# A selective scan's last states: B, C and the scan's outputs placed in the room of K and V

## The chip, the cores and the metric

The kernel runs on one core of one Trainium2 chip, as one launch. The metric is the device time of that core in microseconds (us); where several runs were made, the median is given. The profile is of one separate execution, with its own time.

## What is computed

Two layers run one after the other on x of shape (4, 128, 64, 64), 4 images of 128 channels and 4096 pixels. The first is an attention of 4 heads over the 4096 pixels of an image, with a residual and a layer norm. The second adds three things: a 3 x 3 convolution, a product in the Fourier domain, and a Mamba block, which is where the change lies. Cut to what matters here:

```
y = layernorm(x + softmax(Q K^T / sqrt(32)) V Wo + bo)      # per image, 4 heads of 32
xs = silu(conv1d(in_proj(y)));  dt, B, C = split(x_proj(xs)); dt = softplus(dt_proj(dt))
h0 = 0                                                       # per image, 256 channels x 16 states
h  = exp(dt * A) * h + dt * B * xs                           # pixel after pixel, 4096 of them
y' = sum over the 16 states of (h * C) + xs * D
out = conv3x3(y) + fourier(y) + out_proj(y' * silu(z))
```

## The kernel before

**Tiles and stages.** An image's 4096 pixels are cut into 8 chunks of 512 (`NCH`, `L`), so there are 32 chunks (`CHUNKS`). The attention works on halves: one chunk of queries with one pair of heads, 64 of them (`HALVES`), each against 32 tiles of 128 keys (`NT`). The outer loop at L985 counts steps t; half H takes steps 32 H to 32 H + 31, so the attention ends at t = 2048. In each step it issues the matmuls of one key tile: `scores_for_exp` (L478, reads K), `scores_for_max` for the next half (L434, reads K), `times_values` (L498, reads V).

**The order of the work.** All else is fitted in between by hand. Short jobs (generators) are due at given steps, and a `Plan` (L100) lets so many of them advance in each step; after the attention it lets up to four of each kind. The order of instructions on each engine is therefore fixed when the kernel is built; each engine takes its own in order and waits by semaphores for the others. DMAs of the attention and the scan are issued by SP, also in order.

**K and V.** `KK` (L311) holds 2 x 8 tiles of 128 x 512, one per pair of heads and chunk, and `VA` (L314) 8 tiles of 128 x 528. They are reloaded for each image, and after step 2048 nothing uses them.

**The scan.** It runs `LAG` = 144 steps behind: chunk c starts at t = 144 + 64 c. A chunk has 32 states v: n = v // 2 is the state's number in the reference (0 to 15), hf = v % 2 the half of the 256 channels. Each takes two steps:
- `scan_load` (L769) brings rows n of B and of C, broadcast over the 128 partitions, from the DRAM tile `bcd` that `scan_bc` (L694) wrote: one DMA of 512 KB into `bc`, of which there are three buffers. It is issued three n ahead (L1012).
- `scan_decay` (L774), ACT: dA = exp(dt * A), into PSUM. In the tail two PSUM buffers take turns.
- `scan_input_term` (L782): db = u * B, on POOL (GpSimd) during the attention, on DVE (VectorE) after it. It stands two states ahead of its scan.
- `scan_state` (L787): the scan itself on DVE (L793), from `state` into one of two `hs` buffers; a copy of its last column to `state` on POOL (L796); the product with C on POOL (L797), in place; then the sum over n. For most chunks POOL adds into `acc` (L812). For the last two chunks (30 and 31), which lie after the attention, PE adds with an identity matmul into PSUM (L806).

`mamba_input` (L619) begins a chunk; at an image's first chunk it sets `state` and the convolution's `carry` to zero on POOL. In the instruction order that memset stands among the states of the chunk before it. `scan_output` (L890) gates the sums, multiplies by the output weights (L914), adds (L920) and, for the second half of an image, adds the flipped Fourier part that `load_flipped` brought (`wr`; additions L887, L888 on POOL). `flips` (L932) does this addition later for the first half of an image, with loads of `ob` and `wr` and a store; for the last image these four (chunks 27 to 24) fall into the tail.

**The tail.** After step 2048 there remain the last states of chunk 29, all of chunks 30 and 31 (t = 2064 to 2191), chunk 31's whole input side (`mamba_input`, `scan_dt`), two gates, a convolution (L857), three `scan_output` and the four flips.

Of the kernel before, what the change touches and what calls it, by code (L numbers as in the profile page):

```python
# [9 lines left out]
F32 = mybir.dt.float32  # L10
F32R = mybir.dt.float32r
AF = mybir.ActivationFunctionType
ALU = mybir.AluOpType
# [4 lines left out]
P = 128  # L18
# [5 lines left out]
L = 512  # L24
# [3 lines left out]
NH = DI // P  # L28
NS = 16
# [126 lines left out]
def attention_then_conv_mamba(  # L156
# [17 lines left out]
    nc = tc.nc  # L174
    ctx.enter_context(tc.manual_schedule())
    B, C, N = x.shape
    NCH = N // L
    NT = N // P
    CHUNKS = B * NCH
    HALVES = CHUNKS * PAIRS  # L180
    SCALE = float(HD) ** -0.5

    const = ctx.enter_context(tc.tile_pool(name="const", bufs=1))
    att = ctx.enter_context(tc.tile_pool(name="att", bufs=2))
    loc = ctx.enter_context(tc.tile_pool(name="loc", bufs=2))
# [9 lines left out]
    for h in range(HEADS):  # L195
        k, j = divmod(h, 2)
# [3 lines left out]
    for h in range(HEADS):  # L200
        k, j = divmod(h, 2)
        c = COL["bk"] + k
# [9 lines left out]
    for h in range(HEADS):  # L212
        k, j = divmod(h, 2)
        c = COL["bq"] + h
# [16 lines left out]
    for h in range(HEADS):  # L231
        row = h % 2 * HS
        hs = slice(h * HD, (h + 1) * HD)
# [19 lines left out]
    def col(name, k=0):  # L253
        return vec[:, COL[name] + k : COL[name] + k + 1]
# [5 lines left out]
    sel = const.tile([P, P], F32R, name="sel")  # L260
    ones = const.tile([P, 1], F32, name="ones")
    nc.vector.memset(ones, 1.0)
    minus_one = const.tile([P, 1], F32, name="minus_one")
    nc.vector.memset(minus_one, -1.0)
    g = const.tile([P, 3, P], F32, name="g")
# [10 lines left out]
    def constants_of_the_rest():  # L276
# [34 lines left out]
    KK = [  # L311
        [const.tile([P, L], F32R, name=f"K_{k}_{i}") for i in range(NCH)] for k in range(PAIRS)
    ]
    VA = [const.tile([P, TPC, HEADS, HD + 1], F32, name=f"V_{i}") for i in range(NCH)]  # L314
# [4 lines left out]
    state = const.tile([P, NH * NS], F32, name="state")  # L319
# [5 lines left out]
    plan = Plan(2, {"x": 2, "f": 1})  # L325

    def bank_tile(bank, shape, name):
        return psum.tile(shape, F32, tag=f"m{bank}", name=name)
# [285 lines left out]
    xps, xss, dts, us, accs, gates, xds, bcds = ({} for _ in range(8))  # L614

    def inner(c):
        return xps[c][:, 1 : RPC + 1, 1 : W + 1]

    def mamba_input(c):  # L619

        i = c % NCH
        while c not in XH:
            yield ""
        yield ""
        xp = loc.tile([P, RPC + 2, W + 2], F32, tag="xp", name=f"xp_{c}", bufs=2)
        xps[c] = xp
        nc.gpsimd.memset(xp[:, :, 0 : W + 2 : W + 1], 0.0)
        if i == 0:
            nc.gpsimd.memset(xp[:, 0, 1 : W + 1], 0.0)
            nc.gpsimd.memset(state, 0.0)  # L630
            nc.gpsimd.memset(carry, 0.0)
        if i == NCH - 1:
            nc.gpsimd.memset(xp[:, RPC + 1, 1 : W + 1], 0.0)
        bank = yield "PB"
        pt = bank_tile(bank, [P, TPC, P], f"pt_{c}")
        for t in range(TPC):
            nc.tensor.transpose(pt[:, t, :], XH[c][:, t, :], ident)
        yield "A"
        plan.release(bank)
        nc.scalar.activation(  # L640
            inner(c),
            pt.rearrange("p t (r w) -> p (t r) w", w=W),
            AF.Identity,
            scale=col("gamma"),
            bias=col("beta"),
        )
        if i:
            nc.scalar.activation(xp[:, 0, 1 : W + 1], xps[c - 1][:, RPC, 1 : W + 1], AF.Copy)
            nc.scalar.activation(xps[c - 1][:, RPC + 1, 1 : W + 1], xp[:, 1, 1 : W + 1], AF.Copy)
            edges.add(c - 1)  # L650
        if i == NCH - 1:
            edges.add(c)

        xss[c], dts[c], us[c] = {}, {}, {}
        for hf in range(NH):
            plan.now(1, scan_input(c, hf))
        plan.now(2, spectral(c))
# [108 lines left out]

    dA, db, bcs, scaled = {}, {}, {}, set()

    def scan_load(c, n):  # L769
        bc = loc.tile([P, 2, L], F32, tag="bc", name=f"bc_{c}_{n}", bufs=3)  # L770
        nc.sync.dma_start(bc, bcds[c][n::NS, :].partition_broadcast(P))
        bcs[c, n] = bc

    def scan_decay(c, v):  # L774
        n, hf = divmod(v, NH)
# [6 lines left out]
    def scan_input_term(c, v, engine):  # L782
        n, hf = divmod(v, NH)
        db[c, v] = loc.tile([P, L], F32, tag="db", name=f"db_{c}_{hf * NS + n}")
        engine.tensor_tensor(db[c, v], us[c][hf], bcs[c, n][:, 0, :], ALU.mult)  # L785

    def scan_state(c, v):  # L787

        n, hf = divmod(v, NH)
        k = hf * NS + n  # L790
        assert (c, hf) in scaled
        hs = loc.tile([P, L], F32, tag="hs", name=f"hs_{c}_{k}")
        nc.vector.tensor_tensor_scan(  # L793
            hs, dA.pop((c, v)), db.pop((c, v)), state[:, k : k + 1], ALU.mult, ALU.add
        )
        nc.gpsimd.tensor_copy(state[:, k : k + 1], hs[:, L - 1 :])  # L796
        nc.gpsimd.tensor_tensor(hs, hs, bcs[c, n][:, 1, :], ALU.mult)  # L797
        if c >= CHUNKS - 2:

            if v == 0:  # L800
                late = psum.tile([P, NH, L], F32, tag=f"s{CHUNKS - c}", name=f"acc_{c}")
                for h in range(NH):
                    accs[c, h] = late[:, h, :]
            if n == 0:
                nc.tensor.matmul(accs[c, hf], ident, xss[c][hf], start=True, stop=False)
            nc.tensor.matmul(accs[c, hf], ident, hs, start=False, stop=n == NS - 1)  # L806
        elif n == 0:
            acc = loc.tile([P, L], F32, tag=f"acc{hf}", name=f"acc_{c}_{hf}")
            accs[c, hf] = acc
            nc.gpsimd.tensor_tensor(acc, xss[c][hf], hs, ALU.add)  # L810
        else:
            nc.gpsimd.tensor_tensor(accs[c, hf], accs[c, hf], hs, ALU.add)  # L812
# [3 lines left out]
    def spectral(c):  # L816

        b, i = divmod(c, NCH)
        bank = yield "PB"
        p1 = bank_tile(bank, [P, TPC, P], f"p1_{c}")  # L820
        for t in range(TPC):
            nc.tensor.matmul(p1[:, t, :], XH[c][:, t, :], hilbert, start=True, stop=True)
        yield "A"
        plan.release(bank)
        hx = loc.tile([P, L], F32, tag="hx", name=f"hx_{c}", bufs=2)
        hxs[c] = hx
        nc.scalar.activation(
            hx, p1.rearrange("p t c -> p (t c)"), AF.Copy, scale=col("gamma")
        )
        bank = yield "PB"  # L830
        pw = bank_tile(bank, [P, RPC, W], f"pw_{c}")
        nc.tensor.matmul(pw, g_flip, inner(c), start=True, stop=False)
        yield "P"
        nc.tensor.matmul(
            pw.rearrange("p r w -> p (r w)"), g_fliphil, hx, start=False, stop=True
        )
        yield "A"
        plan.release(bank)
        w = loc.tile([P, L], F32, tag="w", name=f"w_{c}", bufs=1)
        nc.scalar.activation(w, pw.rearrange("p r w -> p (r w)"), AF.Copy)  # L840
        yield ""
        if i == 0:
            wd[b] = dram.tile([P, N], F32, tag="wd", name=f"wd_{b}")
        nc.sync.dma_start(wd[b][:, i * L : (i + 1) * L], w)
# [136 lines left out]
            plan.at((b + 1) * NCH * SLOT + 44 + 10 * i, 4, flips(b * NCH + NCH // 2 - 1 - i))  # L981

    t = 6 - SLOT
    end = (CHUNKS + 3) * SLOT
    while t < end or not plan.idle():  # L985
        H, m = divmod(t, NT)
        if 0 <= H < HALVES:
            scores_for_exp(H, m)
        h1, s1 = divmod(t + LEAD, NT)
        if 0 <= h1 + 1 < HALVES:  # L990
            scores_for_max(h1 + 1, s1)
        H, m = divmod(t - 1, NT)
        last = m == NT - 1
        if last and 0 <= H < HALVES:
            times_values(H, m)
        c, s = divmod(t - LAG, SLOT)
        odd = s % 2 == 1
        if -1 <= c < CHUNKS:
            v = c * STATES + s // 2
            if not odd:  # L1000
                if v >= 0:
                    scan_state(*divmod(v, STATES))
            else:
                if 0 <= v + 1 < CHUNKS * STATES:
                    scan_decay(*divmod(v + 1, STATES))
                if 0 <= v + 2 < CHUNKS * STATES:
                    late = t > HALVES * NT
                    scan_input_term(
                        *divmod(v + 2, STATES), nc.vector if late else nc.gpsimd
                    )  # L1010

                n = v // NH + 3  # L1012
                if s % 4 == 3 and 0 <= n < CHUNKS * NS:
                    scan_load(*divmod(n, NS))
        if t < -LEAD or t > HALVES * NT:
            plan.step(t, {"D": 4, "P": 4, "A": 4})
        elif odd:
            plan.step(t, {"D": 2, "P": 2, "A": 2})
        else:
            plan.step(t, {"D": 0, "P": 0, "A": 1})  # L1020
        if not last and 0 <= H < HALVES:
            times_values(H, m)
        t += 1
# [76 lines left out]
```

## Time and profile before

| | us |
|---|---|
| median of 3 runs | 6248.88 (6247.15 to 6250.07) |
| the profiled execution: its own time | 6247.33 |
| the profiled execution: span from first to last instruction | 6245.5 |
| PE busy | 6001.6 (96%) |
| POOL busy | 4605.3 (74%) |
| DVE busy | 4284.2 (69%) |
| ACT busy | 3582.9 (57%) |
| scans on DVE (L793), 1024 of them | 1305.7, 1.275 each |
| products with C on POOL (L797), 1024 | 1307.0, 1.276 each |
| copies to state on POOL (L796), 1024 | 212.6, 0.208 each |

How to read it: PE is TensorE's matmul queue and PEld its weight loads; ACT is ScalarE, SP the engine that issues DMAs. A group's line names what it writes and reads, its shapes, its count, the busy time, the mean of one, and the idle time of its engine just before, with what ended that idle time after an arrow. The page also cuts the span into 40 equal slices of 156 us and gives busy shares in tenths, with the clock that PE was granted. A wait that is put down to an engine means that its semaphore came last. Idle time on an engine costs something only where that engine holds up the end.

### The profile page before, as it was taken

The numbers are of one execution on the slowest core, as the hardware profiler recorded it, in microseconds if no ns is written. First come the engines' busy times: TensorE is split into PE (matmuls) and PEld (weight loads), VectorE is DVE, ScalarE is ACT, GpSimd is POOL, SyncE is SP. The second block draws the span as 40 slices with busy tenths as digits, with TensorE's granted clock in tenths as the row PEclk, the third lists the DMA queues.
The fourth block names the chain that finished last, engine by engine and source line by source line (L and its number), as shares of the span: only waits on it lengthen the run. The fifth ranks groups of instructions, "written<-read, shape, count | busy, mean of one in ns | idle before, by whom it ended". The sixth has DMA issues, their size and how long they took to land.

```text
span 6245.5 us, 83489 instructions
## 1 busy us (share of the span) xinstructions
PE 6001.6 (96%) x32076; PEld 2540.6 (41%) x32076; DVE 4284.2 (69%) x4405; ACT 3582.9 (57%) x4858; POOL 4605.3 (74%) x4951
## 2 busy tenths in 40 slices
PE   5999999999999999999999999999999999999956
PEld 2444444444444444444444444444444444444321
DVE  4556777777777677777767777767776766677556
ACT  1455666665666656566665556656565655665642
POOL 0006887777888777888887788877788877778866
PEclk7999999999999999999999999999999999999976
DMA  3002222223222222223232222222322222212223
GB/s 111 14 15 60 62 58 58 65 65 103 72 75 58 62 62 63 59 65 84 76 87 62 65 62 65 55 60 70 98 70 63 57 52 56 56 53 55 59 68 93
DMA packets 234225, 404.98 MB, mean 65 GB/s; under 512 B 38872, under 2 KB 40416, under 8 KB 233824
## 3 DMA queue, kind: packets, MB, share of 16 engines
q1 hardware_dynamic: 229440, 397.75, 23.3%
q8 instruction: 251, 4.11, 0.3%
q10 hardware_dynamic: 4384, 1.89, 0.1%
q14 instruction: 150, 1.23, 0.1%
HBM read 350.54 MB, written 49.02 MB: 64 GB/s over the span
## 4 chain that ended last, share of the span: by engine, by line
PE 80%; POOL 9%; DVE 5%; ACT 3%; issue 2%; DMA 1%; ACTq 0%; SPq 0%; POOLq 0%; DVEq 0%
PE po L498 27%; PE s L478 25%; PE s L434 13%; PE pf L857 4%; POOL hs L797 3%; DVE part L441 2%; ACT e L486 2%; DVE hs L793 2%; POOL db L785 1%; PE pi L663 1%; PE pdt L713 1%; POOL acc L812 1%; PE pq L410 1%; PE pd L699 1%; PE py L554 1%
## 5 line engine op out<-in xcount | busy, mean ns | idle before, releaser
L441 DVE TENSOR_REDUCE part<-s 128x2 f32<-128x1024 f32 x2048 | 2501.0, 1222 | 1613.6 <-PE s L434 1611.9
L486 ACT ACTIVATE e<-s 128x1024 f32<-128x1024 f32 x2048 | 2094.1, 1023 | 2257.5 <-PE s L478 2249.3
L498 PE MATMUL po<-e,V 128*33 128x512 f32 x8192 | 2160.1, 605 | 2.8 <-DVE oz L508 0.3
L478 PE MATMUL s<-Q,K 64*128 64x512 f32 x8192 | 1500.7, 444 | 25.3 <-ACT e L486 20.2
L793 DVE TENSOR_TENSOR_SCAN hs<-dA,state,db 128x512 f32<-128x512 f32 x1024 | 1305.7, 1275 | 158.9 <-ACT dA L780 69.2
L797 POOL TENSOR_TENSOR hs<-hs,bc 128x512 f32<-128x512 f32 x1024 | 1307.0, 1276 | 82.0
L434 PE MATMUL s<-K,Q 64*128 64x512 f32 x8192 | 1297.7, 395 | 44.4 <-DVE part L441 42.0
L478 PEld LDWEIGHTS s<-Q,K 64*128 64x128 f32 x8192 | 611.5, 185 | 1753.7 <-ACT e L486 1186.1
L785 POOL TENSOR_TENSOR db<-u,bc 128x512 f32<-128x512 f32 x954 | 1223.0, 1282 | 1.6 <-DMA bc<-bcd 1.6
L812 POOL TENSOR_TENSOR acc<-acc,hs 128x512 f32<-128x512 f32 x900 | 1151.7, 1280 | 70.6
L796 POOL COPY state<-hs 128x1 f32<-128x1 f32 x1024 | 212.6, 208 | 976.6 <-DVE hs L793 976.1
L434 PEld LDWEIGHTS s<-K,Q 64*128 64x128 f32 x8192 | 763.7, 186 | 280.5 <-DVE part L441 102.9
L478 PE MATMUL s<-MX,sel 64*128 64x512 f32 x4096 | 810.3, 392 | 0.0
L780 ACT ACTIVATE dA<-dt,negA 128x512 f32<-128x512 f32 x1024 | 702.5, 686 | 146.8 <-DVE hs L793 146.7
L498 PEld LDWEIGHTS po<-e,V 128*33 128x33 f32 x8192 | 299.2, 109 | 899.0 <-issue 865.0
L478 PEld LDWEIGHTS s<-MX,sel 64*128 64x128 f32 x4096 | 383.8, 184 | 90.0
L857 PE MATMUL pf<-xp,cw 128*128 128x512 f32 x576 | 288.2, 617 | 0.0
L450 POOL COPY wide<-mx 128x128 f32<-128x128 f32 x256 | 63.2, 292 | 196.9 <-DVE mx L447 196.9
L806 PE MATMUL acc<-hs,cst 128*128 128x512 f32 x128 | 110.8, 969 | 86.7 <-POOL hs L797 86.7
L531 POOL TENSOR_TENSOR oz<-oz,rz 128x512 f32<-128x512 f32 x64 | 81.9, 1279 | 106.7 <-DMA rz<-rd 106.7
L857 PEld LDWEIGHTS pf<-xp,cw 128*128 128x128 f32 x576 | 96.1, 188 | 131.9 <-issue 126.9
L554 PE MATMUL py<-wat_vo,oz 128*128 128x128 f32 x512 | 83.0, 285 | 22.6 <-POOL oz L531 18.6
(134 smaller groups left out, 3561.0 us busy)
## 6 DMA issues: line engine op xcount, KB each, us to landing
bc<-bcd SPq DMA_DIRECT2D x512, 512.0 KB
K<-kd SPq DMA_DIRECT2D x64, 256.0 KB
rz<-rd SPq DMA_DIRECT2D x128, 128.0 KB
vd<-vst SPq DMA_DIRECT2D x32, 264.0 KB
V<-vd SPq DMA_DIRECT2D x32, 264.0 KB
xq<-in_x SPq DMA_DIRECT2D x32, 256.0 KB
xk<-in_x SPq DMA_DIRECT2D x32, 256.0 KB
kd<-khi SPq DMA_DIRECT2D x32, 256.0 KB
```

The costliest lines, as they stand in the source:

```text
L434: nc.tensor.matmul(sc[:, j, :], QT[H][rows[j], n, t * P : (t + 1) * P], KK[k][m][rows[j], :], start=n == 0, stop=n == 1,)
L441: nc.vector.tensor_reduce(part[H][:, t, :, m], sc, AX.X, ALU.max)
L478: nc.tensor.matmul(s[:, j, :], sel[rows[j], :] if n == 2 else KK[k][i][rows[j], t * P : (t + 1) * P], mov[rows[j], :], start=n == 0, stop= ...
L486: nc.scalar.activation(e, s, AF.Exp)
L498: nc.tensor.matmul(po[H][used[j], :], VA[i][:, t, 2 * k + j, :], e[:, j, :], start=m == 0, stop=m == NT - 1,)
L780: nc.scalar.activation(dA[c, v], dts[c][hf], AF.Exp, scale=negA[:, k : k + 1])
L785: engine.tensor_tensor(db[c, v], us[c][hf], bcs[c, n][:, 0, :], ALU.mult)
L793: nc.vector.tensor_tensor_scan(hs, dA.pop((c, v)), db.pop((c, v)), state[:, k : k + 1], ALU.mult, ALU.add)
L796: nc.gpsimd.tensor_copy(state[:, k : k + 1], hs[:, L - 1 :])
L797: nc.gpsimd.tensor_tensor(hs, hs, bcs[c, n][:, 1, :], ALU.mult)
L812: nc.gpsimd.tensor_tensor(accs[c, hf], accs[c, hf], hs, ALU.add)
L857: nc.tensor.matmul(pf, cw[:, k, :], xps[c][:, dy : dy + RPC, dx : dx + W], start=k == 0, stop=False)
```

## The change

It does three things.
1. Room for B and C. From step 2017 on, when no buffer of the three-deep ring is free, `scan_load` takes two tiles of K or V instead, one for the row of B and one for the row of C, filled by two DMAs of 256 KB. There are ten such pairs: four of the first pair of heads' K (from step 2017), four of the second's (from 2060), two of V tiles 4 to 7 (from 2068). A pair goes back to the list six steps after its last use is issued. A load is now issued as soon as there is room and `bcd` is there, at most one in each odd step, not at fixed three n ahead. In the built program 25 of the loads go to K and V.
2. Room for hs. In chunks 30 and 31 the scan writes into V tiles 0 to 3 in turn, so four buffers in place of two.
3. The first state. An image's first chunk scans from a constant zero tile; the memsets of `state` are gone, and the last chunk of each image does not copy its last column to `state` (128 copies in all).

On PE, ACT and DVE the instructions stand in the same order as before, with one memset more on DVE. POOL has 132 fewer, SP 25 more.

```diff
+    zero = const.tile([P, 1], F32, name="zero")
+    nc.vector.memset(zero, 0.0)
...
-            nc.gpsimd.memset(state, 0.0)
...
+    spare = [((HALVES - 1) * NT + 1, KK[0][i : i + 2]) for i in range(0, NCH, 2)]
+    spare += [(HALVES * NT + 12, KK[1][i : i + 2]) for i in range(0, NCH, 2)]
+    spare += [(HALVES * NT + 20, VA[i : i + 2]) for i in range(4, NCH, 2)]
+    taken, ring = {}, [3]
+
+    def flat(t):
+        return t.bitcast(F32) if len(t.shape) == 2 else t.rearrange("p t h d -> p (t h d)")[:, :L]
+
     def scan_load(c, n):
-        bc = loc.tile([P, 2, L], F32, tag="bc", name=f"bc_{c}_{n}", bufs=3)
-        nc.sync.dma_start(bc, bcds[c][n::NS, :].partition_broadcast(P))
-        bcs[c, n] = bc
+
+        if ring[0]:
+            ring[0] -= 1
+            bc = loc.tile([P, 2, L], F32, tag="bc", name=f"bc_{c}_{n}", bufs=3)
+            nc.sync.dma_start(bc, bcds[c][n::NS, :].partition_broadcast(P))
+            bcs[c, n] = [bc[:, k, :] for k in range(2)]
+        else:
+            taken[c, n] = spare.pop(0)[1]
+            bcs[c, n] = [flat(t) for t in taken[c, n]]
+            for k in range(2):
+                nc.sync.dma_start(
+                    bcs[c, n][k].unsqueeze(1),
+                    bcds[c][k * NS + n : k * NS + n + 1, :].partition_broadcast(P),
+                )
...
-        engine.tensor_tensor(db[c, v], us[c][hf], bcs[c, n][:, 0, :], ALU.mult)
+        engine.tensor_tensor(db[c, v], us[c][hf], bcs[c, n][0], ALU.mult)
...
-        hs = loc.tile([P, L], F32, tag="hs", name=f"hs_{c}_{k}")
+        if c >= CHUNKS - 2:
+            hs = flat(VA[v % 4])
+        else:
+            hs = loc.tile([P, L], F32, tag="hs", name=f"hs_{c}_{k}")
         nc.vector.tensor_tensor_scan(
-            hs, dA.pop((c, v)), db.pop((c, v)), state[:, k : k + 1], ALU.mult, ALU.add
+            hs,
+            dA.pop((c, v)),
+            db.pop((c, v)),
+            state[:, k : k + 1] if c % NCH else zero,
+            ALU.mult,
+            ALU.add,
         )
-        nc.gpsimd.tensor_copy(state[:, k : k + 1], hs[:, L - 1 :])
-        nc.gpsimd.tensor_tensor(hs, hs, bcs[c, n][:, 1, :], ALU.mult)
+        if c % NCH < NCH - 1:
+            nc.gpsimd.tensor_copy(state[:, k : k + 1], hs[:, L - 1 :])
+        nc.gpsimd.tensor_tensor(hs, hs, bcs[c, n][1], ALU.mult)
+        if hf == NH - 1 and (c, n) in taken:
+            spare.append((plan.t + 6, taken.pop((c, n))))
+        elif hf == NH - 1:
+            ring[0] += 1
...
+    loaded = 0
...
-                n = v // NH + 3
-                if s % 4 == 3 and 0 <= n < CHUNKS * NS:
-                    scan_load(*divmod(n, NS))
+                if loaded < CHUNKS * NS and loaded // NS in bcds:
+                    if ring[0] or spare[0][0] <= t:
+                        scan_load(*divmod(loaded, NS))
+                        loaded += 1
```

## The prediction

> **What bounds the kernel now.** I read the page first: its slices, then its chain.
>
> ```profile
> PE   5999999999999999999999999999999999999956
> POOL 0006887777888777888887788877788877778866
> PEclk7999999999999999999999999999999999999976
> ```
>
> For 37 of 40 slices TensorE is full, at 9 or more tenths and full clock; in the last two it drops to 5 and 6 tenths and its clock to 7 and 6. Nothing in the full part waits for the tiles that this change touches, so the change can pay only after the attention has ended, near 5990 us. Next I cut that tail into stretches (columns: window, its length, busy time and count of PE, PEld, DVE, ACT, POOL, then the granted clock, the DMA share, GB/s).
>
> ```profile
> 6004.00:6097.00 93.00, 54.31 (x94) 19.49 (x95) 55.33 (x57) 35.40 (x64) 54.96 (x63) 0.72 0.26 70
> 6097.00:6134.00 37.00, 23.18 (x27) 5.88 (x26) 26.14 (x26) 8.99 (x13) 27.11 (x31) 0.64 0.55 153
> 6134.00:6174.00 40.00, 29.23 (x55) 11.32 (x54) 25.49 (x27) 13.58 (x22) 23.59 (x26) 0.84 0.42 98
> 6174.00:6232.00 58.00, 41.34 (x42) 10.31 (x42) 40.18 (x41) 13.15 (x20) 40.11 (x43) 0.53 0.31 77
> ```
>
> In the stretch from 6174 PE, DVE and POOL are all busy for 40 to 41 of 58 us: no engine is the bound, so a loop through all three is. The timeline of 6193 to 6200 shows it.
>
> ```profile
> 6193.96 1.28 DVE L793 TENSOR_TENSOR_SCAN hs<-dA,state,db 128x512 f32<-128x512 f32 x1 [0.74 <-PE acc L806]
> 6195.28 0.69 DVE L785 TENSOR_TENSOR db<-u,bc 128x512 f32<-128x512 f32 x1
> 6195.31 0.71 POOL L796 COPY state<-hs 128x1 f32<-128x1 f32 x1 [0.70 <-DVE hs L793]
> 6196.09 1.26 POOL L797 TENSOR_TENSOR hs<-hs,bc 128x512 f32<-128x512 f32 x1
> 6196.84 1.28 DVE L793 TENSOR_TENSOR_SCAN hs<-dA,state,db 128x512 f32<-128x512 f32 x1 [0.87 <-PE acc L806]
> 6197.41 2.08 PE L806 MATMUL acc<-hs,cst 128*128 128x512 f32 x2 [0.68 <-POOL hs L797]
> 6199.59 1.28 DVE L793 TENSOR_TENSOR_SCAN hs<-dA,state,db 128x512 f32<-128x512 f32 x1 [0.74 <-PE acc L806]
> ```
>
> A scan writes hs, POOL copies its last column and multiplies it by C, PE adds it to acc; only then may the next scan but one write the same of the two hs buffers: 6199.59 - 6193.96 = 5.63 us for two states, 2.815 each. The wait tables put 38.0 us of DVE idle before the scan down to "PE acc" over the tail: 17.0 in 6174:6232, 13.0 in 6097:6134, 5.0 in 6004:6097, some 3 in the rest. The first of these:
>
> ```profile
> DVE hs L793 <- PE acc L806: 17.0, 17, 1.7
> ```
>
> Counted back from the last scan, chunk 30's states v0 to v31 scan from 6004.03 to 6132.8, chunk 31's from 6134.28 to 6231.88.
>
> **What the Trainium skill says.** (1) "SBUF — State Buffer", section "Who interferes with whom": a DVE instruction with two SBUF inputs contends with a GpSimd one that reads SBUF, and whoever comes first blocks the other; with at most one it doesn't. The trace agrees: the copy beside db takes 0.71 us, alone 0.18; the multiply beside the scan (dA lies in PSUM) stays at 1.26. So db and POOL's work take turns. (2) "TensorE: Matmul & The Clock Gate", section "What's actually happening": the clock is half after an idle window of some 3.4 us and full after a busy one. The trace agrees in kind: acc takes 2.07 us here, 1.12 at 6127.42 after a dense pair.
>
> **The change, part by part.**
> *hs in V's room, four buffers for two.* The program order of PE, ACT and DVE is otherwise the same in both programs' instruction lists (the zero tile's memset apart), and the 64 scans of the last two chunks do write V. The loop of 5.63 us then spans four states, 1.41 each, below the engines' own pace. That pace I take from scans that did not wait: 6140.93 to 6142.85 is 1.92 (1.28 scan, 0.69 db, overlapping slightly). POOL keeps it: multiplies at 6174.52 and 6176.45 are 1.93 apart, copy and blocked time included. PE's half-clock work follows itself 1.87 to 1.99 apart (6070.82 to 6072.69, and before). I take 1.93. Bounds: 1.90, if nothing ever collides; 2.15 if db, copy and multiply never overlap (0.69 + 0.18 + 1.26 and gaps).
> - *From v11 of chunk 31 on* (6174.32 to 6230.60) there are 20 intervals with nothing else on the path: 56.3 before, 20 x 1.93 = 38.6 after: **-17.7** (bounds -13.3 to -18.3).
> - *6004 to 6097.* The 5.0 us of waits here do not count. POOL is busy without a break from 6078.65 to 6096.68, behind the three operations of scan_dt and the gate; before that, PE's convolution (7.0 us from 6049.77) and ACT's queue (dA behind xd, behind pd on PE: 10.3 us of DVE idle to 6062.76) hold the scan. An earlier scan only waits for these: **0**. If that cover were gone it would be -5.0, in rival (d).
> - *6097 to v1 of chunk 31.* DVE no longer waits, so POOL is next. From the end of v18's multiply (6096.68) it has 15 states (v19 to v1) at 1.93 = 29.0 and three flip additions at 1.25 + 0.2 = 4.4: it ends at 6130.0 where it ended at 6140.45, -10.5. But POOL then arrives earlier at the flip of chunk 25, whose ob and wr loads stand on SP behind a bc load that needs v23's multiply, in both orders. From that multiply's end (6111.66) to the addition (6118.53) were 6.9 us; two states between take 3.9, so POOL stalls 3.0. Together **-7.5** (bounds -4.5, if two flips stall 3.0 us, to -10.5, if none does).
> - *6140 to v11.* The gate's and the convolution's matmuls, with ACT's dA queued behind (3.1 us at 6161.60, 5.0 at 6171.99), are the path and stay: **0**, though DVE shows 1.1 of hs wait at 6156.47 that they cover.
>
> *B and C in K and V, 13 slots for 3.* It removes the wait of the SP queue for POOL (148.7 us in the tail), but DVE waited for a bc only once there, 0.3 us: **-0.3 to 0**, 0 taken. It adds: 25 of the loads become two DMAs of one row each, the same bytes; SP spends 0.4 us more on each, 10 us over some 300. What is queued behind a load on SP: the loads of rz, wr and ob, and the stores. For rz of half 62 two K loads (0.8 us) go between rd and rz; POOL uses rz 5.3 us after its issue, so it is hidden. wr of chunk 29 moves about 1 us back from 6006.90 and is needed at 6023.07: hidden. At 1.93 us a state the loads want 512 KB in 3.86 us, 136 GB/s; the stretch from 6097 already moved 153 at a DMA share of 0.55. So supply should hold.
>
> *State copies of each batch's last chunk, and the memsets, gone; zero as first state.* 128 copies of 0.18 to 0.7 us on POOL. Around chunks 7 and 15 (1880 to 2250 and 3290 to 3660 us) PE was busy for 368.5 of 370 us: nothing. In chunk 23 PE idles for some 4 us behind POOL bursts with about nine copies: up to -2.5; I take **-1**. In chunk 31 they lie in DVE's shadow. At the very end the last copy goes (0.18 and a gap of 0.08): **-0.2**. The scan's pointer to zero instead of state costs nothing.
>
> *PE's clock at the end.* After v31: acc 2.07, two output matmuls 3.75 us, at half clock. PE will be nearly full at half clock for 39 us and may be granted the full one: -2.9 at most, nothing at least; I take **-1**.
>
> Sum: -17.7 - 7.5 - 1 - 0.2 - 1 = -27.4. On the profiled execution's own 6247.33 (span 6245.5) that gives 6219.9; the median of the runs is 1.55 above it: **6221.5**.
>
> **Rivals.**
> (a) *Port and flips take the wait's place.* db and POOL's work never overlap (2.15 a state: -13.3), and the flips eat all of the middle stretch: 6248.9 - 13.3 = 6235.5. For it: POOL's 0.65 to 0.71 us copies, and the one wait on ob (1.2 us). Against: back-to-back pairs at 1.93. 10%.
> (b) *Nothing comes of it*: the supply of B and C is the limit as soon as DVE runs faster. Against: DMA share of 0.31 in the last stretch. Within 3 us of 6249. 4%.
> (c) *Slower: POOL stalls in the flips.* With twice the DMAs in flight, ob and wr land late; POOL, in order, holds every multiply and four states later the scan. It decides from 27 us of new stalls: four flips at 10 us each, against 6.9 from release to use now, give 6248.9 - 27 + 40 = 6262. Against: only one bc load is newly due ahead of each. 4%.
> (d) *More*: all hs waits go, the clock rises, chunk 23 gains fully: -18.3 - 10.5 - 5.0 - 2.5 - 2.9 = -39.2, 6210. 7%.
> That the buffers are not used as told is excluded by the instruction lists.
>
> **How the numbers follow.** My forecast, 6213 to 6232, has 75%: from -18.3 - 10.5 - 2.5 - 0.2 - 2.9 = -34.4 and some room, to -13.3 - 4.5 = -17.8. The range takes in (a): 6213 to 6236, leaving 15%. Under 6236.4 the time is lower by 0.2%, about what can be told from no change: forecast, (a) and (d) make 92%, less 4% for an (a) that ends above it. So 0.88, 0.08, 0.04.
>
> **What would show it.** Scans of the last 20 states 1.92 to 1.95 us apart, with no "PE acc" wait in front; the same start of chunk 30 and the same gap near 6052 to 6062; a longer wait of the addition L887 for ob; chunk 31 without copies. Wrong: states still 2.5 us or more apart, waits of db on the K and V loads, or POOL stalls over 5 us a flip.

## The result, and the profile after

The changed kernel takes 6231.01 us (median of 8 runs, 6226.95 to 6236.14) where the kernel before takes 6249.92 (8 runs, 6247.15 to 6253.70). The ratio is 0.9970 with an interval of 0.9959 to 0.9981, so 18.9 us are gained (12 to 26). Three runs of the changed kernel lie at 6235.3 to 6236.1 us and five at 6227.0 to 6232.4. The profiled execution of after is the longest of the eight: its own time is 6236.14, its span 6234.4. So places and stretches below are read in single executions, and totals are taken from medians.

The page's slices of after: the last two are what the change was to alter.

```profile
PE   5999999999999999999999999999999999999966
POOL 0005887778887777888787888777788777778877
PEclk7999999999999999999999999999999999999987
```

In the last two slices PE goes from 5 and 6 tenths to 6 and 6, POOL from 6 and 6 to 7 and 7, the granted clock from 7 and 6 to 8 and 7. To compare stretches one must first find the same events again. Chunk 30's first scan starts at 6020.8 in after and at 6004.0 in before, so the tail begins 16.7 us *later*. The stretches of before, moved to the same scans (columns as before: window, length, busy time of PE, PEld, DVE, ACT, POOL, granted clock, DMA share, GB/s):

```profile
6021.00:6114.00 93.00, 53.89 (x92) 19.73 (x92) 52.83 (x57) 33.83 (x62) 53.33 (x62) 0.70 0.44 128
6114.00:6145.00 31.00, 19.11 (x27) 6.16 (x28) 25.78 (x26) 10.25 (x16) 26.37 (x31) 0.75 0.57 141
6145.00:6184.00 39.00, 29.61 (x56) 11.35 (x56) 25.61 (x28) 13.60 (x23) 22.95 (x18) 0.87 0.36 97
6184.00:6222.00 38.00, 24.86 (x38) 6.46 (x38) 37.35 (x40) 13.45 (x20) 35.11 (x21) 0.87 0.00 1
```

The last line holds the gain: 38 us for 20 states where before took 56.3, and DVE is busy for 37.4 of the 38. The loop through three engines is gone and one engine is the bound. The DMA share is 0.00: with 13 slots the last rows of B and C had all arrived before 6184. The timeline of that stretch (start, length, engine, line, what it does, in brackets the idle time before it and what ended it):

```profile
6201.91 1.28 DVE L817 TENSOR_TENSOR_SCAN V<-dA,state,db 128x512 f32<-128x512 f32 x1
6203.17 1.12 PE L840 MATMUL acc<-V,cst 128*128 128x512 f32 x2 [0.80 <-POOL V L827]
6203.22 0.69 DVE L806 TENSOR_TENSOR db<-u,bc 128x512 f32<-128x512 f32 x1
6203.27 1.77 POOL L827 TENSOR_TENSOR V<-V,K 128x512 f32<-128x512 f32 x1 [0.15 <-DVE V L817]
6203.83 1.28 DVE L817 TENSOR_TENSOR_SCAN V<-dA,state,db 128x512 f32<-128x512 f32 x1
```

The scans stand 1.92 us apart with no wait in front; POOL's multiply is stretched from 1.26 to 1.77 while db runs, and costs nothing. Over the whole tail DVE's waits for the scan are now these two:

```profile
DVE V L817 <- ACT dA L801: 30.4, 9, 7.1
...
DVE V L817 <- PE acc L840: 3.8, 1, 3.8
```

Of 38.0 us of waits for PE one of 3.8 is left. The waits for dA on ACT grew from 19.1 us in before to 30.4: part of what was removed had been covered by them. Scan to scan, from the two profiled executions (v is a state of chunk 30 or 31; differences are taken before rounding):

| stretch | before | after | difference | predicted |
|---|---|---|---|---|
| chunk 30 v0 to v19 | 93.4 | 94.2 | +0.8 | 0 |
| chunk 30 v19 to chunk 31 v3 | 45.4 | 38.6 | -6.8 | -7.5 |
| chunk 31 v3 to v11 | 31.5 | 31.0 | -0.4 | 0 |
| chunk 31 v11 to v31 | 56.3 | 37.7 | -18.6 | -17.7 |
| chunk 31 v31 to the end | 14.9 | 12.0 | -2.9 | -1.2 |
| the tail | 241.5 | 213.6 | -27.9 | -26.4 |

The tail did what was forecast. But the whole gained 18.9, so some 9 us were given back before the tail begins, where -1 was forecast. That is the question of the experiments.

The place can be read from one DMA that is issued once a half (the load of `zc`, line 519 in before and 521 in after). After minus before, in us from the span's start:

| half | 0 | 15 | 31 | 47 | 62 | 63 |
|---|---|---|---|---|---|---|
| after | +2.8 | +9.1 | +12.8 | +17.8 | +17.2 | +13.4 |

The +2.8 at half 0 isn't the change's: every other kernel's trace stands 0.8 to 4.2 us behind this trace of before there. From there the loss grows through most of the attention, in halves that have nothing to do with the last chunks, and small falls interrupt it. So it is in the main a slower pace, not an event. (The fall at half 63 is lost again before chunk 30's first scan, at +16.7.) Over 400 to 5900 us, first before, then after (busy time over the recorded matmuls, mean ns of one, PE's idle time):

```profile
L478 PE MATMUL s<-Q,K 64*128 64x512 f32 x7662 | 1403.6, 444 | 21.5 <-ACT e L486 17.4
L434 PE MATMUL s<-K,Q 64*128 64x512 f32 x7604 | 1193.7, 392 | 30.3 <-DVE part L441 27.8
L478 PE MATMUL s<-MX,sel 64*128 64x512 f32 x3830 | 757.5, 392 | 0.0
```

```profile
L480 PE MATMUL s<-Q,K 64*128 64x512 f32 x7636 | 1401.8, 445 | 17.7 <-ACT e L488 15.3
L436 PE MATMUL s<-K,Q 64*128 64x512 f32 x7612 | 1217.4, 397 | 27.1 <-DVE part L443 25.6
```

One matmul, the scores for the maximum (s<-K,Q), is 5 ns longer and fills 23.7 us more of PE, and PE waits no more than before. Nothing of the change touches it, except one thing: `zero` is a new tile of 4 bytes a partition, which takes 32 in the built program. It is laid ahead of the attention's tiles, K, V, `oz` (the outputs), Q, MX (the maxima) and e (the exponentials), and all of them begin 32 bytes later. Counted from a multiple of 64 bytes K and V go from 0 to 32, and Q, MX and e from 32 to 0.

My theory was now: the tail is as forecast, and the zero tile's shift costs some 16 us of attention, against 6 to 8 that the rest of the change gains there. The rivals: loads of B and C ahead of time cost it, or the tail's parts are worth less together than apart.

### The profile page after: what moved, and what is told of

Its sections match the earlier page's. It is cut to its first block, busy times and chain, and to the rows that moved or that the text cites. A ratio compares the mean times of both kernels' runs of the same rounds, so it can differ in the third digit from the quotient of the medians.

```text
span 6234.4 us, 83338 instructions
## 1 busy us (share of the span) xinstructions
PE 6005.2 (96%) x32076; PEld 2540.9 (41%) x32076; DVE 4286.5 (69%) x4406; ACT 3585.0 (58%) x4858; POOL 4579.0 (73%) x4819
## 5 line engine op out<-in xcount | busy, mean ns | idle before, releaser
L436 PE MATMUL s<-K,Q 64*128 64x512 f32 x8192 | 1322.2, 400 | 41.2 <-DVE part L443 39.6
L827 POOL TENSOR_TENSOR hs<-hs,bc 128x512 f32<-128x512 f32 x952 | 1215.5, 1277 | 177.5 <-DVE hs L817 108.6
L817 DVE TENSOR_TENSOR_SCAN hs<-dA,state,db 128x512 f32<-128x512 f32 x832 | 1060.7, 1275 | 86.0 <-ACT dA L801 54.0
L826 POOL COPY state<-hs 128x1 f32<-128x1 f32 x864 | 160.2, 185 | 844.8 <-DVE hs L817 844.8
L817 DVE TENSOR_TENSOR_SCAN hs<-dA,zero,db 128x512 f32<-128x512 f32 x128 | 163.2, 1275 | 7.7 <-POOL db L806 7.4
L840 PE MATMUL acc<-V,cst 128*128 128x512 f32 x128 | 90.1, 807 | 78.2 <-POOL V L827 78.0
```

The source lines that it names most:

```text
L436: nc.tensor.matmul(sc[:, j, :], QT[H][rows[j], n, t * P : (t + 1) * P], KK[k][m][rows[j], :], start=n == 0, stop=n == 1,)
L817: nc.vector.tensor_tensor_scan(hs, dA.pop((c, v)), db.pop((c, v)), state[:, k : k + 1] if c % NCH else zero, ALU.mult, ALU.add,)
L827: nc.gpsimd.tensor_tensor(hs, hs, bcs[c, n][1], ALU.mult)
```

## The experiments

All runs stand beside runs of the kernel before on the same chip, whose medians lay between 6249.9 and 6250.4. Gains and losses are taken against the before that ran beside the kernel in question. "The tail" is the time from chunk 30's first scan to the end in the profiled execution; it is 241.5 in before. A gain ahead of the tail is the gain in medians less the tail's in one profiled execution. Executions of one kernel differ by 3 to 10 us, so such remainders are rough.

**The zero tile alone.** The kernel before with the tile, which nothing uses:

```diff
     ones = const.tile([P, 1], F32, name="ones")
     nc.vector.memset(ones, 1.0)
+    zero = const.tile([P, 1], F32, name="zero")
+    nc.vector.memset(zero, 0.0)
```

> The kernel before with one thing added: the constant zero tile (128 x 1) and its memset, used by nothing. It moves every SBUF tile allocated after it, K, V, Q and all of the scan's among them, up by 32 bytes, as in the changed kernel. Theory A (the shift costs PE some 0.2 us a half of the attention, which is what ate a third of the tail's gain): slower than before by 8 to 17 us, 6258 to 6267, with the mean of the scores' matmul s<-K,Q near 0.396 us where before it was 0.389 in the same window. Rival B (the drift of the profiled run is the spread between runs): no difference to before, 6250, and 0.389.

Measured: 6267.0 (6 runs), ratio 1.0029 (1.0018 to 1.0041): 16.6 us slower, at the upper end of theory A, with a tail of 242.1. A tile of 4 bytes that no instruction reads costs nearly what the whole change gained, and all but 0.6 us of it lies ahead of the tail. The matmul, in the window of 400 to 5900 us as above:

```profile
L436 PE MATMUL s<-K,Q 64*128 64x512 f32 x7608 | 1216.5, 397 | 28.1 <-DVE part L443 26.6
```

**The change without the shift.** The zero put beside the ones, in the 32 bytes that their tile takes anyway:

```diff
-    ones = const.tile([P, 1], F32, name="ones")
+    pair = const.tile([P, 2], F32, name="ones")
+    ones, zero = pair[:, 0:1], pair[:, 1:2]
     nc.vector.memset(ones, 1.0)
-    zero = const.tile([P, 1], F32, name="zero")
     nc.vector.memset(zero, 0.0)
```

> The changed kernel with the zero column put beside the ones in that tile's 32 bytes, so that K, V and Q stand where they stood before. Theory A: all of the tail's 27 us show, 6219 to 6224, and s<-K,Q is back at 0.389 us. Rival B: as the changed kernel, 6228 to 6236.

Measured: 6216.06 (5 runs), ratio 0.9946 (0.9934 to 0.9959): 34.4 us gained, 15.0 us less time than the changed kernel. The tail is 215.1, so 26.4 of the gain lie there. The matmul is back at before's pace:

```profile
L436 PE MATMUL s<-K,Q 64*128 64x512 f32 x7608 | 1194.0, 392 | 28.9 <-DVE part L443 26.5
```

The two runs agree on the shift, 15.0 and 16.6, with opposite edits. The remaining 8.0 are a gain in the attention; it is more than theory A took, so the time fell 3 us below its range.

**hs in V alone.** The kernel before, with only the second part:

```diff
-        hs = loc.tile([P, L], F32, tag="hs", name=f"hs_{c}_{k}")
+        if c >= CHUNKS - 2:
+            hs = VA[v % 4].rearrange("p t h d -> p (t h d)")[:, :L]
+        else:
+            hs = loc.tile([P, L], F32, tag="hs", name=f"hs_{c}_{k}")
```

> The kernel before with the scan's outputs of the last two chunks in V tiles 0 to 3 (four buffers) and nothing else; B and C keep the ring of three, addresses are as before. The prediction gave B and C's room 0 us, so by it this should have nearly all of the tail's gain: 6223 to 6226. Rival C (with faster states the three-deep ring becomes the limit: a load is released by the multiply of its slot's last user and takes some 5.5 us to land, which makes 13.2 us for six states, 2.2 each where 1.93 would go): db waits for bc, states 2.1 to 2.3 us apart at the end, 6229 to 6235.

Measured: 6231.46 (7 runs), ratio 0.9971 (0.9961 to 0.9982): 19.0 gained, as rival C expected, and the tail is 222.5, 19.0 shorter. The last 20 states take 43.8 us, 2.19 each and not 1.88. The timeline names what stands in the way:

```profile
6197.24 1.27 DVE L796 TENSOR_TENSOR_SCAN V<-dA,state,db 128x512 f32<-128x512 f32 x1
6199.83 0.89 DVE L785 TENSOR_TENSOR db<-u,bc 128x512 f32<-128x512 f32 x1 [1.32 <-DMA bc<-bcd]
6200.64 1.27 DVE L796 TENSOR_TENSOR_SCAN V<-dA,state,db 128x512 f32<-128x512 f32 x1
```

and the wait table from 6097 to the end its sum:

```profile
DVE db L785 <- DMA bc<-bcd: 13.1, 9, 3.7
```

In before DVE waited once for a bc, 0.3 us. With the hs loop open, the three bc buffers are the next limit: the load of a new row waits on SP for a multiply, and then takes its time to land. The one issued at 6194.86 let the product above start at 6199.83, 5.0 us later.

**B, C and the state part, hs as before.** The kernel of the second experiment with hs in its two buffers:

```diff
-        if c >= CHUNKS - 2:
-            hs = flat(VA[v % 4])
-        else:
-            hs = loc.tile([P, L], F32, tag="hs", name=f"hs_{c}_{k}")
+        hs = loc.tile([P, L], F32, tag="hs", name=f"hs_{c}_{k}")
```

> The changed kernel with hs back in its two buffers for all chunks, zero in the tile of ones (addresses of K, V and Q as before); B and C in K and V, no state copies in each image's last chunk. The prediction: 0 from B and C's room, about -1 from the copies, so 6247 to 6250, with states 2.8 us apart at the end. Rival C says the same here: the room matters only once hs no longer holds the scan.

Measured: 6238.35 (21 runs), ratio 0.9982 (0.9975 to 0.9988): 12.1 gained, tail 236.0. That is over 8 us below what the prediction and rival C gave. It is to be read beside the state part alone, two experiments further on.

**Both rooms, without the state part.** The changed kernel with the memsets, the copies and the scan's start from `state` restored, and no zero tile:

```diff
-    zero = const.tile([P, 1], F32, name="zero")
-    nc.vector.memset(zero, 0.0)
...
+            nc.gpsimd.memset(state, 0.0)
...
-            state[:, k : k + 1] if c % NCH else zero,
+            state[:, k : k + 1],
...
-        if c % NCH < NCH - 1:
-            nc.gpsimd.tensor_copy(state[:, k : k + 1], hs[:, L - 1 :])
+        nc.gpsimd.tensor_copy(state[:, k : k + 1], hs[:, L - 1 :])
```

> The changed kernel without its third part: memsets of state, the first state from state and all 1024 copies as before, no zero tile, so addresses of K, V and Q as before. B, C and hs have their new room. Theory D (the 128 copies and the memsets were in PE's way during the attention, which the prediction put at 1 us): it loses the 4 to 6 us that the kernel with zero beside the ones gained in the attention, keeps the gain of the last 32 steps and of the tail: 6220 to 6224. Rival E (the early loads of B and C give the attention's gain): 6215 to 6218.

Measured: 6219.7 (5 runs), ratio 0.9954 (0.9942 to 0.9967): 30.2 gained, tail 216.1. The time lies between the ranges of theory D and rival E, so it doesn't decide between them; the traces do, in the next experiment. Against hs alone it is 11.8 lower, of which 6.4 lie in the tail, where the waits for bc are gone. Against the change without the shift it is 3.6 higher: that is the state part, once both rooms are there, and only 1.0 of it lies in the tail. The intervals of the two overlap, so 3.6 is rough.

**The state part alone.** The kernel before with the third part, the zero beside the ones:

```diff
-            nc.gpsimd.memset(state, 0.0)
...
-            hs, dA.pop((c, v)), db.pop((c, v)), state[:, k : k + 1], ALU.mult, ALU.add
+            hs, dA.pop((c, v)), db.pop((c, v)), state[:, k : k + 1] if c % NCH else zero, ALU.mult, ALU.add
...
-        nc.gpsimd.tensor_copy(state[:, k : k + 1], hs[:, L - 1 :])
+        if c % NCH < NCH - 1:
+            nc.gpsimd.tensor_copy(state[:, k : k + 1], hs[:, L - 1 :])
```

> The kernel before with the third part alone (no memset of state, zero as the first state, no copies in each image's last chunk; zero lies in the tile of ones, addresses as before). Theory D: 4 to 6 us in the attention, and about 5 in chunk 31, where with two hs buffers the copy (0.26 us with its gap, 20 states) is on the loop from scan to scan: 6238 to 6242. The prediction's own numbers: -1 in the attention and -0.2 in the tail, so 6249. Rival E: -5 from chunk 31 alone, 6245.

Measured: 6239.31 (21 runs), ratio 0.9982 (0.9976 to 0.9989): 10.6 gained, as theory D expected and some 10 us more than the prediction's own numbers. The tail is 237.1, 4.4 shorter: with two hs buffers the copy is a link of the loop (scan, copy, multiply, add), and chunk 31 takes 2.57 us a state without it, not 2.815. The loop itself stays, as the waits from 6170 to 6230 show:

```profile
DVE hs L794 <- PE acc L808: 12.1, 15, 1.4
```

The other 6 us lie in the attention. The traces show such a gain apart from the medians. From half 0's load of `zc` to chunk 30's first scan, four kernels with this part and K and Q in their old places take 5784.0 to 5788.2 us, and six without it, the two rooms with the copies kept among them, take 5788.1 to 5793.4: 5.5 less in the mean. So the gain comes with this part, and the early loads of B and C alone bring none there (5793.4 with both rooms and the copies kept). Two places can be told. Around chunk 7 (from half 16's load to half 20's) it is 366.5 to 366.6 us with this part and 367.4 to 368.9 without, and around chunk 23 (half 48 to half 53) 469.8 to 470.4 and 470.8 to 473.4. Where the rest lies, and how a copy on POOL holds PE up there, is not shown. With B's and C's room added, the fourth experiment gains 1.0 us more than this one, within the intervals: while two hs buffers bind, that room is worth nothing that can be seen.

**A shift of 64 bytes.** An unused tile of 16 elements a partition in the zero tile's place:

```diff
+    pad = const.tile([P, 16], F32, name="pad")
+    nc.vector.memset(pad, 0.0)
```

> The kernel before with an unused tile of 128 x 16 (64 bytes a partition) where the zero tile stands in the changed kernel; all later tiles move by 64 bytes. If any move of the tiles costs what 32 bytes cost: 6267. If it is where a tile starts within 64 bytes that counts: 6250, and s<-K,Q at 0.389 us. A gain would say that 128 bytes matter.

Measured: 6251.84 (13 runs), ratio 1.0003 (0.9995 to 1.0011). Every tile behind it moves twice as far, and the time stays, with s<-K,Q at 392 ns: it is the place within 64 bytes that counts.

**K alone moved by 32 bytes.** An unused tile of 4 bytes ahead of K and one behind it, so that V, Q, MX and e move by 64:

```diff
+    pad0 = const.tile([P, 1], F32, name="pad0")
+    nc.vector.memset(pad0, 0.0)
     KK = [
         [const.tile([P, L], F32R, name=f"K_{k}_{i}") for i in range(NCH)] for k in range(PAIRS)
     ]
+    pad1 = const.tile([P, 1], F32, name="pad1")
+    nc.vector.memset(pad1, 0.0)
```

> The kernel before with an unused 128 x 1 tile ahead of K and another behind it: K starts 32 bytes further on, V, Q and everything later 64. If K as the streamed operand of s<-K,Q is what suffers: 6264 to 6268 and 0.396 us, as with the zero tile. If it is another tile (Q, e, the scan's): 6250.

Measured: 6253.94 (13 runs), ratio 1.0007 (0.9998 to 1.0015): 4.0 more, which the interval can't tell from nothing, and far from the 14 to 18 that were expected if K alone suffers.

**All but K moved.** Only the second of these two tiles:

> The kernel before with an unused tile of 4 bytes a partition between K and V, so that K stays where it was and V, oz, state, Q, MX, e and all behind them begin 32 bytes later (V 32, Q, MX and e 0 bytes past a multiple of 64, where they were 0, 32, 32, 32). The zero tile shifted all of them and cost 16.6 us; K alone shifted cost some 4. If the cost lies in V, Q or e: 6262 to 6266. If it needs K out of place too (K and Q together): 6247 to 6252. If K and Q both at a multiple of 64 is the best place of all: below 6246, with the matmul s<-K,Q under 389 ns.

Measured: 6249.24 (13 runs), ratio 0.9997 (0.9989 to 1.0005). No cost, as expected if K must be out of place too.

**All behind V moved.** The same tile behind V:

> The kernel before with the same unused tile behind V: K and V stay, and oz, state, Q, MX, e and the rest begin 32 bytes later. Against the run that shifts V too it tells V apart: if V matters (the products with e read it as weights or as data), this one stands nearer to 6250 than that; if Q, MX or e matter, both show the same time. I expect the same time as that run, within 3 us.

Measured: 6247.99 (13 runs), ratio 0.9997 (0.9989 to 1.0005). The same as the run that moves V too, as expected, so with K in place V's start doesn't matter. And neither run costs anything: V, Q, MX or e out of place alone don't carry it.

**K and everything behind it moved.** Only the first of the two tiles, so the small constants between the ones and K stay where they were:

> The kernel before with the unused tile directly ahead of K: K and everything behind it begin 32 bytes later, as with the zero tile, but the small constants between the ones and K (minus_one, g, the spectral bias, A, bo) stay. K alone cost 4 us and all but K nothing, though each made the matmul s<-K,Q 2 ns longer (394 for 392 ns). If K and Q out of place together cost the 16.6 us: 6264 to 6268, with that matmul at 396 to 397 ns. If the small constants bring the rest: 6248 to 6256.

Measured: 6268.1 (6 runs), ratio 1.0032 (1.0019 to 1.0044): 18.1 slower. So the constants don't matter, and it takes both: K at 32, and of what lies behind K the tiles that then stand at 0 past a multiple of 64 (Q, MX and e). The matmul from the same view and window as above, one kernel each: K alone, all but K, behind V, and both:

```profile
L438 PE MATMUL s<-K,Q 64*128 64x512 f32 x7608 | 1206.7, 394 | 29.6 <-DVE part L445 27.4
```

```profile
L480 PE MATMUL s<-Q,K 64*128 64x512 f32 x7664 | 1398.9, 443 | 21.2 <-ACT e L488 17.2
L436 PE MATMUL s<-K,Q 64*128 64x512 f32 x7608 | 1206.7, 394 | 30.0 <-DVE part L443 27.6
L480 PE MATMUL s<-MX,sel 64*128 64x512 f32 x3832 | 753.6, 389 | 0.0
```

```profile
L436 PE MATMUL s<-K,Q 64*128 64x512 f32 x7604 | 1206.6, 394 | 29.9 <-DVE part L443 27.3
```

```profile
L480 PE MATMUL s<-Q,K 64*128 64x512 f32 x7636 | 1401.4, 445 | 18.6 <-ACT e L488 16.1
L436 PE MATMUL s<-K,Q 64*128 64x512 f32 x7608 | 1215.7, 396 | 28.0 <-DVE part L443 26.5
L480 PE MATMUL s<-MX,sel 64*128 64x512 f32 x3818 | 754.8, 392 | 0.0
```

Each of the two moves adds 13 us to this matmul and both together 22 us. With all but K moved, others give it back: divided by the recorded count and multiplied by all (8192, 8192, 4096), s<-K,Q is 13.3 us above before, s<-Q,K 5.4 below and s<-MX,sel 4.6 below, +3 in sum and nothing in the kernel's time. With both moved they are 23.0 above, 2.7 above and 0.4 below, +25, and the kernel is 18 slower. The ends of matmuls are modelled in a profile, so these sums give the direction and the rough size.

**K and V first.** The second experiment's kernel, with a free pair of K or V taken ahead of a free buffer of the ring:

```diff
-        if ring[0]:
+        if ring[0] and not (spare and spare[0][0] <= plan.t):
...
-                    if ring[0] or spare[0][0] <= t:
+                    if ring[0] or (spare and spare[0][0] <= t):
```

> The changed kernel with its zero beside the ones (6216.06) and with the room in K and V taken before the three buffers of the ring. A K or V pair comes free six steps after its last use is issued, so the loads of ob and wr for the flips no longer stand on SP behind a bc load that waits for a multiply just issued. If that load is what makes POOL wait 3.2 us for wr at the addition of chunk 25 (and 0.4 at chunk 24), both waits go and the time is 6212 to 6213.5. If wr's own transfer is what takes the time (the DMA engines are busy there), the wait stays and the time is 6216, within 1.5. Slower than 6218 if loads that now run earlier delay rd and rz of the last half.

Measured: 6214.84 (5 runs), ratio 0.9944 (0.9931 to 0.9956), 1.2 below the second experiment, within the intervals; tail 214.7 for 215.1. POOL's wait for wr at the flips was 3.6 us in two in the second experiment, 3.2 of it at chunk 25, and is this here:

```profile
POOL ob L921 <- DMA wr<-wd: 4.1, 1, 4.1
```

The wait has moved. In the second experiment a bc load that SP held back 4.4 us for POOL stood ahead of chunk 25's ob and wr, and loads into K that it didn't hold stood ahead of chunk 24's. Here it is the other way round: at chunk 25 the loads into K ahead are held 0.3 us, and POOL waits 0.9 us for ob and not at all for wr; at chunk 24 a bc load is held 3.1 us, and the 4.1 us lie there. So the wait went where the held bc load went, and as a gain in time the attempt failed. Of all kernels run, these two, the change with its zero beside the ones, are the fastest.

## Why the prediction was right, and where it was not

The median, 6231.0, lies in the range and inside the likeliest case's own 6213 to 6232, but 9.5 us above the predicted 6221.5. Two errors of opposite sign lie in it, both in the attention: a cost of 15.0 us that was not seen, and some 5 us more gain than the 1 forecast. That the second softened the first is luck. By these terms alone (-27.9 + 15.0 - 1, an estimate) the time would have been 6236.0, at the very end of the range.

**hs in V, chunk 31 from v11 on.** Right: 1.92 us between scans, -18.6 for -17.7. The pace that I read from scans that did not wait was the one that came. The last scan follows without a db ahead of it, after 1.19 us, so 20 intervals took 37.7 and not 38.6.

**6097 to v1 of chunk 31.** Right in mechanism and size. POOL is next, and stalls at the flips. These are POOL's addition for chunk 25 and SP's queue ahead of it:

```profile
6130.03 1.72 POOL L827 TENSOR_TENSOR V<-V,K 128x512 f32<-128x512 f32 x1
6135.12 1.25 POOL L921 TENSOR_TENSOR ob<-ob,wr 128x504 f32<-128x504 f32 x1 [3.37 <-DMA wr<-wd]
```

```profile
6127.93 0.37 SPq L784 DMA_DIRECT2D bc<-bcd  x1
6128.35 0.47 SPq L971 DMA_DIRECT2D ob<-ymd  x1
6128.86 0.43 SPq L912 DMA_DIRECT2D wr<-wd  x1
```

The stall is 3.4 us, forecast 3.0, and 0.5 more at chunk 24's; the bc load stands directly ahead of ob and wr, as told. The stretch gave -6.8 for -7.5. SP waited 4.4 us for POOL before it issued that load. That this wait is the cause is borne out by the run that takes K and V first: POOL's long wait went from chunk 25 to chunk 24 together with the held bc load.

**6004 to 6097, and 6140 to v11.** Right: +0.8 and -0.4. The 5.0 us of hs waits in the first stretch were covered indeed, and rival (d), which counted them, fell. The 10.3 us of DVE idle to 6062.76, which I put down to dA, were ended by ln_z, one place ahead of dA in ACT's queue; that changes nothing.

**B and C in K and V.** The 0 was right of before's own waits and is wrong as a value of this part. With two hs buffers it is about 0 (1.0 us between two experiments, within their intervals); with hs in V it is 6.4 us of tail, because three bc buffers then bind. Rival (b) named that limit, and the run with hs alone shows it, at 13.1 us of waits; in the whole change the first part removes it. My sum stands only since it took the supply as given: the sentence "supply should hold" carried the worth of the part that I had set at 0.

**PE's clock at the end.** Right in mechanism, the term too small: -2.9 with the last copy, for -1.2; the two bounds together, 2.9 and 0.2, nearly came. In all five kernels with hs in V this stretch takes 12.0 to 12.5 us, in the nine others 13.7 to 14.9. The four output matmuls and the last two of acc, in before:

```profile
6233.52 2.08 PE L806 MATMUL acc<-hs,cst 128*128 128x512 f32 x2 [0.79 <-POOL hs L797]
...
6236.47 3.75 PE L914 MATMUL py<-acc,outw 128*128 128x512 f32 x4 [0.88 <-DVE acc L901]
```

and the output matmuls in after:

```profile
6227.02 1.95 PE L948 MATMUL py<-acc,outw 128*128 128x512 f32 x4 [0.88 <-DVE acc L935]
```

1.95 us for 3.75. The clock was not only full at the end: already in the stretch from 6184 it was 0.87 for 0.53, and acc took 1.12.

**State copies and memsets.** The term of -1 in the attention was too small. Alone the part gained 10.6, of which 4.4 came from a loop that the whole change opens in another way, and the rest lies in the attention; inside the whole change it is worth 3.6 (two kernels whose intervals overlap, so the size is not sure). The sentence that failed is "PE was busy for 368.5 of 370 us: nothing": its first window began at 1880 us, 94 after chunk 7's first scan in before, and from half 16 to half 20 (1645 to 2014 us in before) the traces with this part are 1.2 us shorter in the mean. Around chunk 23 they are 2.3 shorter, where I took 1. The rest is not placed.

**The zero tile, priced as one memset.** This is the step that failed. I set the tile apart as one memset more and the scan's pointer to it at nothing, and never asked which tiles it moves. Its cost is 15.0 to 16.6 us: the largest term after the hs loop. It was also the case for "slower" that I lacked. With that tile, a change that gains less than some 16 us ends above before; the state part alone, worth 10.6, would by these figures, though that was not run. The account: -27.9 in the tail (profiled executions), +15.0 for the shift (medians, changed kernel against the zero beside the ones) and -6.0 for the rest of the attention, found as the remainder to -18.9; the second experiment gives -8.0 for the same rest, and the traces with and without the state part differ by 5.5 there.

**Rival (a)**, port and flips in the wait's place, would have given 6235.5, and the measured median is nearer to it than to 6221.5. The time alone would have favoured it. The trace excludes it: 1.92 us between scans where (a) needs 2.15, and 3.8 us of stalls where (a) lets them eat 10.5. **Rival (c)** needed 27 us of new stalls, and there were 3.8.

## What to carry to other kernels

When a change allocates anything on chip, even four bytes, compare the addresses of all tiles behind it, and put small constants into a tile that exists or behind the large ones. When a total disagrees with the stretch that the change was made for, align the two traces on one event that recurs in every stage: a difference that grows evenly is a pace, and a pace is looked for in the mean of the commonest instruction. A buffer that no wait shows is worth what the next limit is worth once the present one is gone, so parts of one change are priced together and in order.

## What the runs showed of the hardware

- The time of an f32 matmul with 64 rows depended on where K and the tiles behind it begin in SBUF: s<-K,Q took 392 ns with K at 0 and Q at 32 past a multiple of 64 bytes, 394 with K and Q both at 0 or both at 32, and 396 to 397 with K at 32 and Q at 0. A move of both by 64 bytes left 392. For the kernel only the last could be told from nothing, 15 to 18 us in 6250.
- That Q, and not V, oz, MX or e, is the partner of K is likely, since that matmul reads only K and Q, but Q was not moved by itself. Why the start matters was not found.
- While a VectorE product of two SBUF operands (0.69 us) runs, a GpSimd product that starts beside it takes 1.77 us and not 1.26, and the VectorE one isn't lengthened. This is what the Trainium skill ("SBUF — State Buffer", "Who interferes with whom") says of the one that comes first; in before the VectorE product met the copy, here it meets the large product, and the DVE pace of 1.92 us is the same.
- The acc matmuls on PE, a pair each 2.8 us with gaps of some 0.7, took 2.08 us a pair at a granted clock of 0.53 (6174 to 6232 in before). The same pairs each 1.92 us, with gaps of 0.8, took 1.12 at 0.87 (6184 to 6222 in after).
